# A graph layer on one core: 576 chunks of edges counted in passes of 32 banks instead of 568 in passes of 31, with another plan for interleaving the counted part, and one output buffer instead of two

## The chip, the core and the metric

The kernel runs on one core of one Trainium2 chip. The metric is the device time of one execution in microseconds (us); the number for the kernel before is the median of three runs, 1355.36 us (1352.13 to 1356.22). A profile is one more execution, recorded by the hardware profiler. The engines are PE (TensorE, matrix products; its weight loads are listed apart as PEld), DVE (VectorE), ACT (ScalarE), POOL (GpSimd, which here issues the gathers) and SP (SyncE, which issues most plain transfers).

## What is computed

There are 12,500 nodes with 128 features, 200,000 edges of four types, and one 128x128 weight with a bias for each type:

```python
h = jnp.maximum(_layernorm(x, axis=-1), 0.0)
xs = h[src]
for i in range(4):
    msgs += jnp.where((edge_type == i)[:, None], xs @ W[i] + b[i], 0.0)
return x + jax.ops.segment_sum(msgs, dst, num_segments=12500)
```

The edges are sorted by destination. Destinations are drawn as the square of a uniform number, so the first nodes have very many edges and the last ones few.

## The kernel before

**Chunks.** The edges are cut into 1563 chunks of 128. The first C0 = 568 chunks (all of them edges into about the first 1700 nodes) go the *dense* way, the other TM = 995 the *sparse* way.

**Start.** The normalized features are split into three 16-bit parts and stored to a table in memory, `htab` (98 blocks of 128 rows, 768 bytes a row). Meanwhile the edges of the dense part are sorted into *slots* (`make_slots`). The first three sparse groups (`RAW` = 3, 48 chunks) are gathered from `x` itself, since the table is not ready; part of their work (20 `raw_steps`, emptied three at a time) runs on inside the main loop's first group.

**The sparse way.** The chunks come in groups of G = 16. For each chunk POOL issues one indirect DMA (`gather`, line 591) that brings the 128 rows of its sources from `htab` into a buffer `hm` (10 buffers of two chunks, so at most 20 chunks ahead). DVE builds a one-hot matrix `oh` (line 609), PE multiplies rows by one-hot, three matmuls a chunk (line 644), ACT copies the sums out (line 634), and `weigh` multiplies by the four weights (line 670). DVE adds the result into a ring of running sums (line 733), and finished blocks of 512 nodes leave through `put_out`, `fetch` and `leave`: load `x` (line 751), transpose the ring (line 766), add (line 771), store (line 773). The buffer of this exchange is the tile `xo` of the pool `outp`, which has two buffers.

**The dense way.** For one to three destination nodes at a time, a *bank*, the kernel counts how often each of the 12,500 nodes is a source, by type. A slot (at most 128 edges of a bank) takes two DVE one-hots (`make`, lines 1066, 1070 and 1074) and one matmul of 396 columns (line 1099); ACT turns the counts of a bank into integers (line 1107). Each integer holds three counts as its digits. A *pass* (`multiply`) then multiplies the counts of a batch of banks with the feature table: for each of the 98 table blocks one matmul with the counts read as 8-bit floats and one with counts that ACT decoded (`decode`, line 1167), both of 3 x 4 x banks columns (line 1211). The table blocks stream in through SP (`hs`, line 1195, five buffers of three blocks). UB = 31 is the number of banks in a full batch: 580 banks make 19 batches, the first of 22 and eighteen of 31. The very first pass reads `htab` with three matmuls a block and writes a two-part table `dtab` on the way (`keep`, lines 1181 to 1183), which all later passes read. While a batch is passed, the next one is counted; the first batch has nothing beside it, and the third one (n = 2) is counted alone for its first half, since the pass of the second batch waits for `dtab` (`SETTLE` = 0.5). Where a count runs alone, DVE's one-hots set its pace.

**The order.** PE, DVE and ACT run in the order in which the program is written (`manual_schedule`); SP and POOL are ordered by the scheduler. The main loop (line 1531) goes over the sparse groups from index 3 (`LEAD`) on; between two pieces of a group it takes steps of the generator `dense_work` for as long as the share done is below `pace(gi, part)`. `pace` is a plan in columns: it gives every group the same sum `a_group` of its own columns and dense columns, so that the dense part is done when group FULL - 2 = 58 ends; from index FULL - 1 = 59 on it returns 2.0, which empties whatever is left. Its prices are: 392 columns for a slot, 2.05 x 3 x banks x 392 for a pass and 3.0 x 3 x banks x 392 for the first one.

```python
last = FULL - 1                                  # 1268
a_group = (dense_columns() + sum(own)) / len(own)
...
while work and spent < pace(gi, part):           # 1554
    spent = next(work, None)
```

With TM = 995 there are FULL = 60 groups of 16, then groups of 8, 12, 8, 4 and 3 (index 60 to 64). When the dense part has ended, its memory is freed, buffers `outs` are opened for the last blocks, the four blocks of `acc` (the dense sums) and the blocks still to flush are fetched (lines 1597 to 1608), and the blocks leave while the last groups run.

Of the kernel before, what the change touches and what calls it, by code (L numbers as in the profile page):

```python
# [57 lines left out]
C0 = 568  # L58
UB = 31
# [20 lines left out]
PARTS = 2.05  # L80


@with_exitstack
def kernel(
# [125 lines left out]
    NSLOTS = sum(len(slots_of(u)) for vs in batches for u in vs)  # L210
# [215 lines left out]
    iota_1 = const.tile([P, P], BF16, name="iota_1")  # L426
    nc.vector.tensor_single_scalar(iota_1, iota_b, 1.0, op=ALU.add)
# [25 lines left out]
    ones = const.tile([P, P], F32, name="ones")  # L453
    nc.vector.memset(ones, 1.0)
# [195 lines left out]
    def weigh(t0, g, oh, sb, last):  # L650
# [13 lines left out]
        cnt = spool.tile([P, G * WIN], BF16, name="cnt", bufs=1)[:, : G * win].rearrange("p (g n) -> p g n", g=G)  # L664
# [182 lines left out]
    def check_all():  # L847
# [5 lines left out]
        pb = x_ps.tile([P, 3], F32, name="pt")  # L853
        nc.tensor.matmul(pb, ones, many, start=True, stop=True)
# [19 lines left out]
    def make_slots(dix):  # L874
# [98 lines left out]
        def unpack(a, z, shared):  # L973
# [8 lines left out]
            marks.append(nc.vector.tensor_copy(loT[:, a:z], lo).ins)  # L982
# [59 lines left out]
    def count(now, room):  # L1042
# [18 lines left out]
        def make(n):  # L1061
# [3 lines left out]
            for k, (i, s, by, first, last) in enumerate(sets[n]):  # L1065
# [3 lines left out]
                if by == 1.0:  # L1069
                    one = nc.vector.tensor_scalar(o1[:, k], iota_1, loT[:, s : s + 1], None, ALU.is_equal)  # L1070
                else:
                    if by is None:
                        by = byT[:, s - FIRST : s - FIRST + 1]
                    one = nc.vector.tensor_scalar(o1[:, k], iota_1, loT[:, s : s + 1], by, ALU.is_equal, ALU.mult)  # L1074
# [191 lines left out]
    def pace(gi, part):  # L1266

        last = FULL - 1
        if gi >= last:
            return 2.0  # L1270
        own = [columns(i) for i in range(LEAD, last)]
# [5 lines left out]

    def dense_columns():
        return NSLOTS * float(NB) + sum(3 * len(vs) * (PARTS if i else 3.0) for i, vs in enumerate(batches)) * NW * NT

# [4 lines left out]
    def dense_work():  # L1285


        a_slot = float(NB)
        alone_slot = 3.5 * NB
        a_node = NW * NT  # L1290
        total = dense_columns() + sum(len(slots_of(u)) for u in batches[0]) * (alone_slot - a_slot)
# [3 lines left out]
        for n, vs in enumerate(batches + [None]):  # L1295
# [4 lines left out]
            if vs:  # L1300
                now, first = coming or begin(n)
                coming = None
                steps[first] = sum(len(slots_of(u)) for u in vs) * (a_slot if before else alone_slot)
            if before:
                passed = multiply(before)
                steps[passed] = 3 * len(before[0]) * a_node * (PARTS if before[0] is not batches[0] else 3.0)
# [3 lines left out]
            while done:  # L1310
# [7 lines left out]
                if part is None:  # L1318
                    del done[st]
                    gone += steps[st]  # L1320
# [3 lines left out]
                else:  # L1324
                    done[st] = part
                    yield (gone + sum(done[st] * steps[st] for st in done)) / total
# [432 lines left out]
```

## Time and profile before

| | before |
|---|---|
| median of three runs | 1355.36 us |
| the profiled execution, its own time | 1360.44 us |
| its span in the profile | 1358.7 us |
| busy: PE, PEld | 1243.1 us, 872.8 us |
| busy: DVE, ACT, POOL | 999.0 us, 1066.8 us, 977.8 us |
| gathers from the table (line 591) | 947 |
| slots counted (line 1099) | 1069 |
| casts of counts (line 1107), one for each bank | 580 |

How to read the rows below: a group row gives line, engine, operation, output and inputs by the program's names, the shape, how many (x), the busy time together and the mean of one, and then the idle time just before them with what ended it. A row of windows gives a stretch of time (from and to, in us of the span), its length, and then for each engine the busy time and the number of instructions, the granted PE clock (1.00 is full speed), the share of time in which the DMA engines were busy, and GB/s. A row of waits names who waited, for whom, the total in us, the number of times and the longest. Engine times are as the profiler models them: ends of matmuls overlap, so starts are the safer thing to compare.

### The profile page before, as it was taken

How to read it: one execution, taken by the hardware profiler on the slowest of the kernel's cores; microseconds unless marked ns; L12 is line 12 of the kernel's file. 1: busy time of each engine (PE TensorE's matmuls, PEld its weight loads, DVE VectorE, ACT ScalarE, POOL GpSimd, SP SyncE). 2: the span in 40 equal slices, each digit the busy share in tenths (PEclk: the TensorE clock that was granted, in tenths of full speed). 3: DMA queues.
4: the chain of work that ended last, by engine and by line, in shares of the span. 5: the costliest groups of instructions: out<-in, count | busy, mean ns of one | idle time of the engine just before them, and what ended most of it. 6: DMA issues, size and time to landing. Idle time of an engine off the chain costs nothing.

```text
span 1358.7 us, 30461 instructions
## 1 busy us (share of the span) xinstructions
PE 1243.1 (91%) x9232; PEld 872.8 (64%) x9232; DVE 999.0 (74%) x5139; ACT 1066.8 (79%) x1815; POOL 977.8 (72%) x1024
## 2 busy tenths in 40 slices
PE   5888877999999999999999999999999999998964
PEld 1445654777677766777777676666676666666743
DVE  8996568868888897888776867677676758773552
ACT  6887544889889888898988988888897978886710
POOL 7637463777777777777777777777777777777774
PEclk8885887999999999999999999999999999999977
DMA  7653596888788888888888888887877878778842
GB/s 243 216 204 86 176 338 216 244 272 266 243 256 259 250 255 241 249 257 265 256 259 254 267 249 257 248 246 246 273 227 238 265 214 261 235 234 281 267 122 62
DMA packets 184630, 322.56 MB, mean 237 GB/s; under 512 B 30243, under 2 KB 82524, under 8 KB 184460
## 3 DMA queue, kind: packets, MB, share of 16 engines
q1 hardware_dynamic: 132716, 214.63, 49.0%
q0 software_dynamic: 46992, 96.30, 26.0%
q10 hardware_dynamic: 4752, 9.64, 1.8%
q8 instruction: 73, 1.20, 0.4%
q14 instruction: 97, 0.79, 0.2%
HBM read 294.78 MB, written 25.67 MB: 236 GB/s over the span
## 4 chain that ended last, share of the span: by engine, by line
PE 65%; DMA 12%; DVE 6%; ACT 6%; issue 6%; POOL 4%; DVEq 0%; SPq 0%; ACTq 0%; POOLq 0%
PE pa L1211 35%; PE pt L1099 9%; PE py L670 7%; DMA hm<-htab,srcT 7%; PE ps L644 5%; POOL hm L591 4%; DMA dtab<-dec 2%; DMA hs<-dtab 2%; ACT dec L1167 2%; PE pt L1235 2%; ACT counts L1107 1%; PE ps L702 1%; DVE o L1074 1%; DVE o L1066 1%; PE pt L952 1%
## 5 line engine op out<-in xcount | busy, mean ns | idle before, releaser
L591 POOL DMA_INDIRECT hm<-htab,srcT x947 | 924.3, 976 | 342.1 <-issue 202.5
L1167 ACT ACTIVATE dec<-counts 128x1116 fp32r<-128x1116 uint8 (+1 forms) x594 | 672.2, 1152 | 9.9 <-PE pa L1211 9.0
L1066 DVE TENSOR_SCALAR o<-iota_n,hkT 128x392 bf16<-128x392 f16 x1069 | 354.4, 331 | 180.2 <-PE pt L1099 177.4
L1211 PE MATMUL pa<-dec,hs 128*128 128x372 f32 x1764 | 480.8, 380 | 0.0
L1211 PE MATMUL pa<-counts,hs 128*128 128x372 fp8e4 (+1 forms) x2058 | 435.0, 324 | 22.6 <-DMA hs<-htab 13.8
L1211 PEld LDWEIGHTS pa<-dec,hs 128*128 128x128 f32 x1764 | 309.5, 188 | 41.6 <-issue 0.5
L1107 ACT CAST counts<-pt 128x396 int32<-128x396 f32 x580 | 285.5, 510 | 50.1 <-PE pt L1099 26.2
L1099 PE MATMUL pt<-o,o 128*128 128x396 bf16 x1069 | 285.9, 342 | 15.8 <-ACT counts L1107 9.5
L1211 PEld LDWEIGHTS <-hs 128*128 128x128 f16 (+1 forms) x2058 | 189.6, 98 | 143.1 <-issue 19.4
L644 PE MATMUL ps<-oh,hm 128*128 128x72 bf16 (+7 forms) x2841 | 186.9, 201 | 32.3 <-DMA hm<-htab,srcT 30.9
L1074 DVE TENSOR_SCALAR o<-iota,loT,byT 128x128 bf16<-128x128 bf16 x647 | 216.3, 334 | 0.0
L733 DVE TENSOR_TENSOR ring<-ring,py 128x18 f32 (+6 forms) x912 | 159.0, 174 | 73.1 <-PE py L670 24.1
L644 PEld LDWEIGHTS <-hm 128*128 128x128 f16 x2841 | 136.9, 100 | 103.9 <-DMA hm<-htab,srcT 41.4
L634 ACT ACTIVATE sb<-ps 128x288 f32<-128x288 f32 (+8 forms) x237 | 101.8, 430 | 126.3 <-PE py L670 101.3
L609 DVE TENSOR_SCALAR oh<-iota_b,keyT 128x72 bf16<-128x72 bf16 (+7 forms) x947 | 163.0, 260 | 25.6 <-PE ps L644 24.4
L670 PE MATMUL py<-sb,wsb 128*128 128x288 f32 (+6 forms) x456 | 121.1, 409 | 0.0
L1099 PEld LDWEIGHTS <-o 128*128 128x128 bf16 x1069 | 80.4, 99 | 60.6 <-issue 17.5
L1074 DVE TENSOR_SCALAR o<-iota,loT 128x128 bf16<-128x128 bf16 x422 | 116.7, 277 | 0.0
L670 PEld LDWEIGHTS py<-sb,wsb 128*128 128x128 f32 x456 | 83.3, 193 | 20.7 <-issue 0.3
L575 POOL DMA_INDIRECT hx<-in_x_dram,srcT x48 | 48.0, 1001 | 23.8 <-issue 9.5
L665 ACT CAST cnt<-pt 128x288 bf16<-128x288 f32 (+10 forms) x62 | 25.5, 412 | 39.5 <-PE pt L661 33.6
L509 ACT ACTIVATE h<-hm,nmrt,rstdt 128x128 f32<-128x128 f32 x98 | 42.1, 489 | 0.9 <-DVE mvt L492 0.8
(250 smaller groups left out, 717.8 us busy)
## 6 DMA issues: line engine op xcount, KB each, us to landing
hs<-dtab SPq DMA_DIRECT2D x576, 288.0 KB
hm<-htab,srcT POOLq DMA_INDIRECT x947
htab<-h SPq DMA_DIRECT2D x32, 288.0 KB
hs<-htab SPq DMA_DIRECT2D x32, 288.0 KB
dtab<-dec ACTq DMA_DIRECT2D x32, 288.0 KB
xo<-in_x_dram SPq DMA_DIRECT2D x23, 256.0 KB
out_dram<-xo SPq DMA_DIRECT2D x23, 256.0 KB
hm<-in_x_dram SPq DMA_DIRECT2D x18, 192.0 KB
```

The lines of the kernel that those rows point to most:

```text
L591: one = nc.gpsimd.indirect_dma_start(out=hm[:, (i - h0) * D3 : (i - h0 + 1) * D3], out_offset=None, in_=htab, in_offset=bass.IndirectOffse ...
L609: nc.vector.tensor_scalar(oh[:, i, :], iota_b[:, :K], keyf[:, at : at + 1], None, ALU.is_equal)
L634: nc.scalar.activation(sb[0][:, i0:i1].rearrange("p g t n -> p g (t n)"), ps[:, : i1 - i0, :], AF.Copy, scale=1.0 / UP)
L644: nc.tensor.matmul(ps[:, i - i0, :], rows(i, c), oh[:, i, :], start=(c == 0), stop=(c == 2))
L670: nc.tensor.matmul(py[:, :g, :], wsb[:, t, :], sb[0][:, :g, t, :], start=False, stop=(t == NT - 1))
L733: nc.vector.tensor_tensor(to, to, of(i), ALU.add)
L1066: one = nc.vector.tensor_scalar(o2[:, k, :NB], iota_n, hkT[:, s : s + 1], None, ALU.is_equal)
L1074: one = nc.vector.tensor_scalar(o1[:, k], iota_1, loT[:, s : s + 1], by, ALU.is_equal, ALU.mult)
L1099: one = nc.tensor.matmul(pb, o1, o2, start=first, stop=last)
L1107: lambda i=i, pb=pb: nc.scalar.copy(counts[:, :, i * NT : (i + 1) * NT], pb.rearrange("p (b t) -> p b t", t=NT))
L1167: nc.scalar.activation(decoded[n][:, : j1 - j0, :nv].rearrange("p j (m v) -> p j m v", m=3), by_digit[:, j0:j1, : nu * NT * 4].rearrange(" ...
L1211: nc.tensor.matmul(to if c == 1 and not first else to.rearrange("p (m v) -> p m v", m=3), left, right, start=(j == 0 and c == 0), stop=(js ...
```

## The change

Five things change.

- **More dense chunks, wider passes.** C0 goes from 568 to 576 and UB from 31 to 32. By the formulas of the kernel this makes 596 banks and 1085 slots, still 19 batches (the first of 20 banks, eighteen of 32), and TM = 987 sparse chunks: 60 groups of 16, then 12, 8, 4 and 3. The group of 8 is gone.
- **Another plan.** `pace` runs to `last = FULL`, so the dense part ends with group 59 instead of 58. The prices are new: 4.4 instead of 3.0 for the first pass, 3.5 x 392 for a slot that is counted alone (the first batch, and now also the first half of the third), and 20,000 columns of other work in the loop's first group. The plan now divides by the same total as the work counts itself by.
- **One output buffer.** `outp` has one buffer `xo` instead of two.
- **One-hots compared from 0.** `loT` now holds the low index minus 1, done in the same instruction that converted it, so that `iota_b` serves where `iota_1` (the same plus 1) did; `iota_1` is gone.
- **A table of ones** that only the last check and the fallback path read is made where it is read. A tile of counts, `cnt`, is sized by the widest window in use.

```diff
-C0 = 568
-UB = 31
+C0 = 576
+UB = 32
+FIRST_PASS = 4.4
+ALONE = 3.5
+RAW_WORK = 20000.0
...
-    iota_1 = const.tile([P, P], BF16, name="iota_1")
-    nc.vector.tensor_single_scalar(iota_1, iota_b, 1.0, op=ALU.add)
...
-    ones = const.tile([P, P], F32, name="ones")
-    nc.vector.memset(ones, 1.0)
...
         pb = x_ps.tile([P, 3], F32, name="pt")
+        ones = outp.tile([P, P], F32, name="ones", bufs=1)
+        nc.vector.memset(ones, 1.0)
...
-            marks.append(nc.vector.tensor_copy(loT[:, a:z], lo).ins)
+            marks.append(nc.vector.tensor_single_scalar(loT[:, a:z], lo, -1.0, op=ALU.add).ins)
...
-        last = FULL - 1
+        last = FULL
         if gi >= last:
             return 2.0
-        own = [columns(i) for i in range(LEAD, last)]
+        own = [columns(i) + (RAW_WORK if i == LEAD else 0.0) for i in range(LEAD, last)]
         a_group = (dense_columns() + sum(own)) / len(own)
...
+    def counting_columns(n, part):
+
+        alone = 1.0 if n == 0 else SETTLE if n == 2 else 0.0
+        return sum(len(slots_of(u)) for u in batches[n]) * NB * (part + (ALONE - 1.0) * min(part, alone))
+
+    def passing_columns(n, part):
+        return 3.0 * len(batches[n]) * (PARTS if n else FIRST_PASS) * NW * NT * part
+
     def dense_columns():
-        return NSLOTS * float(NB) + sum(3 * len(vs) * (PARTS if i else 3.0) for i, vs in enumerate(batches)) * NW * NT
+        return sum(counting_columns(n, 1.0) + passing_columns(n, 1.0) for n in range(len(batches)))
...
-                steps[first] = sum(len(slots_of(u)) for u in vs) * (a_slot if before else alone_slot)
+                steps[first] = lambda part, n=n: counting_columns(n, part)
...
-    outp = mid.enter_context(tc.tile_pool(name="outp", bufs=2, side="right"))
+    outp = mid.enter_context(tc.tile_pool(name="outp", bufs=1, side="right"))
```

20 lines of the change are left out of this document (9 added, 11 removed).

## The prediction

> **What bounds the kernel now.** I read the page first, then windows of the gathers, of the matmuls that sum rows, and of all engines, cut where the groups begin; then waits, groups, and the timeline at both ends. From the page:
>
> ```profile
> span 1358.7 us, 30461 instructions
> PE 1243.1 (91%) x9232; PEld 872.8 (64%) x9232; DVE 999.0 (74%) x5139; ACT 1066.8 (79%) x1815; POOL 977.8 (72%) x1024
> PE   5888877999999999999999999999999999998964
> PEclk8885887999999999999999999999999999999977
> L591 POOL DMA_INDIRECT hm<-htab,srcT x947 | 924.3, 976 | 342.1 <-issue 202.5
> ```
>
> PE is full from the eighth slice to the last three, with holes and a lower clock on both sides. POOL looks free by its 72%, but the windows of its gathers (line 591) say otherwise:
>
> ```profile
> 112.00:152.00 40.00, 23.69 (x25) 0.63 0.26 72
> 152.00:262.30 110.30, 63.29 (x62) 0.86 0.82 272
> 262.30:362.00 99.70, 75.92 (x79) 1.00 0.84 262
> 362.00:662.30 300.30, 228.92 (x235) 1.00 0.84 254
> 662.30:1062.30 400.00, 304.32 (x314) 1.00 0.83 251
> 1062.30:1303.70 241.40, 183.16 (x192) 0.98 0.79 243
> 1303.70:1358.70 55.00, 31.34 (x33) 0.69 0.34 90
> ```
>
> From 262 on there is one gather every 1.26 to 1.28 us (400.00 / 314 = 1.274), at the end too, with no room between them; before that one in 1.6 to 1.8. The windows of the summing matmuls (line 644, three a chunk) show the groups:
>
> ```profile
> 112.00:152.00 40.00, 3.39 (x48) 0.63 0.26 72
> 152.00:262.30 110.30, 10.42 (x192) 0.86 0.82 272
> 262.30:362.00 99.70, 12.89 (x240) 1.00 0.84 262
> ...
> 1303.70:1358.70 55.00, 12.46 (x105) 0.69 0.34 90
> ```
>
> 48 matmuls are one group of 16: index 3 takes 40 us, indices 4 to 7 take 110.3 (27.6 each), 8 to 12 take 99.7 (19.9 each). From 362 to 1303.7 lie indices 13 to 59, 941.7 us. The last of them has no dense work:
>
> ```profile
> 1288.85 0.43 PE L644 MATMUL ps<-oh,hm 128*128 128x96 bf16 x6
> ...
> 1301.18 0.95 POOL L591 DMA_INDIRECT hm<-htab,srcT  x1 [0.31 <-issue]
> ...
> 1303.77 0.44 PE L644 MATMUL ps<-oh,hm 128*128 128x104 bf16 x3 [0.46 <-DMA hm<-htab,srcT]
> ...
> 1318.12 3.02 PE L670 MATMUL pt<-sb,wsb 128*128 128x208 f32 x8
> ...
> 1343.85 0.94 POOL L591 DMA_INDIRECT hm<-htab,srcT  x1 [0.30 <-issue]
> ...
> 1351.92 0.44 PE L766 MATMUL pt<-ident,ring 128*128 128x128 f32 x2 [1.68 <-DVE ring L733]
> ```
>
> So 13 to 58 take 1288.7 - 362 = 926.7 us, 20.15 each, and a group of gathers takes 16 x 1.255 (the spacing from 1301.18 to 1343.85, 34 gathers) to 16 x 1.278 (235 in 300.3), 20.1 to 20.4. PE and the gathers run level. The waits of PE's weight loads for gathered rows, in the windows 700 to 900, 900 to 1100 and 1100 to 1285, are small:
>
> ```profile
> PEld L644 <- DMA hm<-htab,srcT: 3.3, 7, 0.8
> ...
> PEld L644 <- DMA hm<-htab,srcT: 7.8, 13, 1.1
> ...
> PEld L644 <- DMA hm<-htab,srcT: 4.7, 5, 2.7
> ```
>
> 15.8 us over the 46 groups, 0.34 each. After 1288.7 no dense work is left to fill PE, and the gathers set the end: the row for index 60 was asked for 2.6 us before PE took it, and the span ends 14.8 us after the last gather.
>
> **The early groups.** By the old plan each group holds 42,611 columns (35,699 dense, 6,912 own), so a planned column costs 20.15 / 42,611 = 0.473 ns in the steady part. Indices 4 to 7 should then take 80.6 us and take 110.3. They hold most of the first pass and the half count that runs alone. The waits of the window 112 to 262 and the one-hots' groups show both:
>
> ```profile
> POOL hm L591 <- PE ps L644: 25.1, 10, 5.0
> PEld L1211 <- DMA hs<-htab: 16.6, 11, 4.3
> ...
> L1066 DVE TENSOR_SCALAR o<-iota_n,hkT 128x392 bf16<-128x392 f16 x1069 | 354.4, 331 | 180.2 <-PE pt L1099 177.4
> ...
> L1074 DVE TENSOR_SCALAR o<-iota,loT,byT 128x128 bf16<-128x128 bf16 x647 | 216.3, 334 | 0.0
> ...
> L1074 DVE TENSOR_SCALAR o<-iota,loT 128x128 bf16<-128x128 bf16 x422 | 116.7, 277 | 0.0
> ```
>
> A slot alone needs 0.61 to 0.67 us of DVE, 1,290 to 1,410 columns at that price, against 392 in the old plan and 1,372 in the new one. The new prices add to indices 4 to 7 about 34,000 columns for the first pass (1.4 x 3 x 22 x 392 less what index 3 did) and 34,300 for the half count, together 32 us; the excess is 29.7. So the new prices fit what those groups cost now.
>
> The new plan gives every group 44,342 columns; index 3 loses 18,269 dense ones (17,430 instead of 35,699). At 0.473 ns that is 8.6 us less for index 3, and indices 4 to 12 take 9 x 20.97 = 188.7 instead of 110.3 + 99.7 = 210.0. Together -30. Following the steps of the generator group by group instead (13 slots in index 3; then 7, 12 and 8 of the 33 steps of the first pass; and so on, each at what such steps take now) I get -26. I take **-28**, bounds 0 (if the rest of the first group's own work, or the clock at 0.63, holds it) and -34. The work is not gone: some 70,000 old-plan columns, 33 us, move behind index 12.
>
> **The steady groups.** 47 groups (13 to 59) now all hold dense work, 1,731 planned columns more each: the wider passes (12 columns more in each of 196 matmuls of a pass), 16 slots more, and the work moved here. The timeline of one pass gives a column's price:
>
> ```profile
> 1286.23 0.81 PE L1211 MATMUL pa<-dec,hs 128*128 128x372 f32 x3
> 1286.88 0.67 PE L1211 MATMUL pa<-counts,hs 128*128 128x372 fp8e4 x3
> 1287.25 0.81 PE L1211 MATMUL pa<-dec,hs 128*128 128x372 f32 x3
> ```
>
> Six matmuls of 372 columns from start to start in 1.02 us, 0.457 ns a column. A group becomes 20.15 + 1.731 x 0.457 - 0.34 (a PE that is slower than the gathers no longer waits for them) = 20.6 us. 47 x 20.6 = 968.2 against 941.7: **+26.5**. Bounds: gathers at 1.255 set the floor, 47 x 20.08, +2; every planned column at 0.473 and no wait recovered gives 20.97, +44. I choose between them by the rows of the passes, which are most of the work.
>
> The Trainium skill, "TensorE: Matmul & The Clock Gate", section "Back-to-back issue gap", gives a warm matmul N / 2.4 ns plus a fixed 2.5 ns. By it an added column costs 0.417 ns, the fixed part nothing, and this term would be +23 instead of +26.5; the row's 0.457 holds also what is fixed per matmul, so it is an upper price for columns that only lengthen matmuls.
>
> The other engines cover their share. ACT and DVE in the window from 362 (busy PE, PEld, DVE, ACT, POOL):
>
> ```profile
> 362.00:662.30 300.30, 294.30 (x2356) 213.21 (x2355) 249.69 (x1303) 265.10 (x419) 228.92 (x235) 1.00 0.84 254
> ...
> 1303.70:1358.70 55.00, 31.76 (x203) 22.23 (x203) 18.41 (x89) 5.79 (x14) 31.34 (x33) 0.69 0.34 90
> ```
>
> ACT is at 88%. 4.8% more dense columns a group (37,430 for 35,699) in 2.2% more time make it 90.5%, DVE 85%: hidden under PE; if ACT bound instead, a group would cost 20.15 x 1.048 = 21.1, just over the upper bound above. The table is streamed 19 times as before, so the DMA load per pass stays.
>
> **The end.** From the start of index 60 the kernel needed 55.0 us for 8 + 12 + 8 + 4 + 3 = 35 chunks. Now 27 are left there, and with PE setting the pace up to index 59 POOL is further ahead: at most 20 chunks (7 x 1.255 + 14.8 = 24 us to the end), or 8 if it only keeps some 10 us (19 x 1.255 + 14.8 = 39). PE itself was busy 31.8 us in that window; less the eight chunks (8 / 35 of the 12.46 us that the same window of line 644 has, 2.8, and the 3.0 us product of that group at 1318) it needs about 26, and with the 6.8 us that follow its last matmul, 33. I take 37, **-18**; bounds 33 (-22) and 45 (only the eight gathers saved, -10).
>
> **One output buffer, and the rest.** A fetch already waits for the store ahead of it to land:
>
> ```profile
> 490.97 0.39 SPq L773 DMA_DIRECT2D out_dram<-xo  x1
> ...
> 495.08 0.38 SPq L751 DMA_DIRECT2D xo<-in_x_dram  x1
> ```
>
> 4.1 us, behind which the table loads of line 1195 queue on SP; PE, five buffers (15 blocks, 30 matmuls, about 5 us) ahead, mostly covers it. With one buffer the fetch waits for the same store. Two places are new. The sums of the raw groups hold the one buffer until their adds in indices 4 to 6 are done, so the first block's fetch, and the table loads behind it, wait for DVE there: 0 to 4 us, taken as 1. At the end, the block due at index 59 is flushed at 61, after the late buffers were dealt out at 60, so its fetch needs one of theirs back: a store and a fetch, 4 to 8 us, while line 771's add holds DVE and behind it the ring adds, one-hots and then PE. The last gathers hide most of it; 1, and 8 without that cover. The removed `iota_1` and `ones` are two short DVE instructions ahead of the loop, `loT`'s subtraction rides in an instruction that exists, 16 more slots widen the slot building by 1.5%: 0. Together **+2**, bounds 0 and 8.
>
> **Sum.** -28 + 26.5 - 18 + 2 = -17.5 on the profiled execution's own 1360.44 us (1.7 outside the span): 1342.9. That execution is 0.4% over the median of the runs; scaled by 1355.36 / 1360.44 the time is **1338 us**, 1.3% faster.
>
> **Rivals.**
> (B) *The gathers set the pace, PE's added columns vanish under them.* For it: the unbroken spacing above, and PE's waits for rows. Against it: PE would have to do 4% more in the same 20.4 us while it is 98% busy. The last gather then comes 28 us earlier for the early groups and 8 x 1.274 = 10.2 earlier for the chunks saved: -38, 1317. The skill's "Perfetto Trace Analysis", section "GPSIMD Engine Instruction", says to time this engine by the spacing of starts, not by its busy span; the windows agree (1.274 us from start to start against a mean of 0.976 busy).
> (C) *The early groups do not get shorter* (the slower side). Place: indices 3 to 12. If the raw steps, the table's round trip through `dtab` and the waits for `hs` set these 250 us rather than the amount of dense work, the thinner plan only pushes 33 us behind. Price 0 instead of -28: +26.5 - 18 + 2 = +10.5, 1366. It decides once less than 10.5 us is gained there. Against it: the excess of 29.7 us that the new prices explain, and 25.1 us in which POOL waited for PE there.
> (D) *The columns cost full price*, 20.97 a group: -28 + 44 - 18 + 2 = 0, 1355. For it: this is the mean price of a planned column now. Against it: that mean holds fixed costs and waits.
> That the plan does not do what it says is a part of D: if dense work slipped past index 59 or the late block stalled the end, the end's gain would be gone, -17.5 + 18, again about 1355.
>
> **Chances.** Forecast 0.62 (its own range 1320 to 1352), B 0.20, C 0.10, D 0.08. About 0.3% is what a measurement of this kernel can tell from no change. Faster: 0.60 of the forecast and B, 0.80; same: D's 0.06 and 0.02 of the forecast, 0.08; slower: C and the rest of D, 0.12. The range 1312 to 1362 takes in most of B and D and leaves out C's centre, and nearly 0.2 in all.
>
> **What would show it.** Index 13 should start near 334 instead of 362, with POOL at 1.28 us a gather from about 230 on; from there 20.6 us a group and hardly a wait for gathered rows; index 60 near 1302, and 37 us from there to the end. If the gathers stay unbroken and PE waits for rows, it is B; if indices 3 to 12 still take 250 us, C; if a group takes 21 us, D. The forecast is wrong if two of the three terms miss by over 10 us in the same direction.

## The result, and the profile after

The changed kernel takes 1347.68 us (median of 20 runs, 1343.2 to 1357.92), the kernel before beside it 1355.64 us (20 runs, 1350.91 to 1359.79): a ratio of 0.9956 with a 95% interval of 0.9938 to 0.9974. It is faster by 0.4%, where 1.3% was forecast. The profiled execution of the change took 1353.06 us, 0.4% over its median, as the one of before was over its own. From the page after:

```profile
span 1351.3 us, 30386 instructions
PE 1248.1 (92%) x9211; PEld 878.6 (65%) x9211; DVE 999.3 (74%) x5154; ACT 1086.2 (80%) x1828; POOL 966.1 (71%) x1016
PE   4878876899999999999999999999999999999995
PEclk9985798789999999999999999999999999999997
L589 POOL DMA_INDIRECT hm<-htab,srcT x939 | 913.3, 973 | 336.2 <-issue 216.3
```

PE stays full to the last slice but one, where before it thinned out over three. The low digits of PE and of its clock at the start are still there. The windows of all engines, cut where each group's first summing matmul starts (from, to, length, then busy PE, PEld, DVE, ACT, POOL, granted PE clock, DMA share, GB/s), are those of index 3, indices 4 to 6 together, each of 7 to 12, indices 13 to 59, and the end:

```profile
108.80:145.20 36.40, 31.34 (x169) 26.04 (x169) 12.97 (x62) 23.79 (x66) 21.54 (x23) 0.50 0.28 73
145.20:211.20 66.00, 50.34 (x488) 38.33 (x487) 49.81 (x233) 34.31 (x85) 47.80 (x48) 0.95 0.86 292
211.20:235.20 24.00, 13.90 (x114) 9.12 (x113) 18.96 (x91) 7.82 (x20) 15.40 (x15) 0.77 0.83 279
235.20:259.80 24.60, 20.85 (x126) 13.61 (x124) 20.69 (x112) 14.18 (x24) 18.50 (x21) 0.67 0.41 110
259.80:278.70 18.90, 18.74 (x154) 13.09 (x152) 17.37 (x89) 17.30 (x28) 14.47 (x15) 1.00 0.86 259
278.70:305.30 26.60, 23.66 (x167) 17.14 (x166) 9.75 (x54) 18.94 (x26) 16.65 (x18) 0.87 0.84 260
305.30:327.00 21.70, 20.93 (x164) 15.05 (x164) 18.28 (x92) 18.74 (x30) 15.47 (x16) 1.00 0.74 219
327.00:345.70 18.70, 18.70 (x152) 13.34 (x151) 15.22 (x78) 17.36 (x28) 14.28 (x15) 1.00 0.84 253
345.70:1313.20 967.50, 947.65 (x7190) 674.71 (x7188) 720.17 (x3762) 845.02 (x1288) 726.68 (x753) 1.00 0.83 251
1313.20:1351.30 38.10, 23.47 (x178) 18.95 (x176) 16.12 (x86) 4.94 (x12) 9.25 (x10) 0.81 0.27 78
```

| | before | forecast | the change's profile |
|---|---|---|---|
| up to index 3 | 112.1 us | | 108.8, -3.3 |
| indices 3 to 12 | 250.0 us | -28 | 236.9, **-13.1** |
| indices 13 to 59 | 941.7 us | +26.5 | 967.5, **+25.8** (20.58 a group) |
| from index 60 | 55.0 us | -18 | 38.1, **-16.9** |
| span | 1358.7 us | -17.5, with +2 for the rest | 1351.3, -7.4 |

Two of the three large terms came out as forecast. The early one came out at half its size. In the rows above the long groups have places: index 3 ran at half clock from end to end (0.50), and indices 7, 8 and 10 took 24.0, 24.6 and 26.6 us at 0.77, 0.67 and 0.87, while 9 and 12 beside them took 18.9 and 18.7 at full clock.

PE sets the pace of the steady part alone. In the waits of weight loads from 345.7 to 1288 the wait for gathered rows is gone but for crumbs (total, times, longest):

```profile
PEld L642 <- DMA hm<-htab,srcT: 7.4, 46, 0.2
```

At the end the late block does wait for its load as forecast, in the waits from 1313.2 on and in SP's queue, but the stores behind it still take 14.3 us to be issued:

```profile
DVE xo L769 <- DMA xo<-in_x_dram: 5.2, 1, 5.2
```

```profile
1325.70 0.39 SPq L771 DMA_DIRECT2D out_dram<-xo  x1
1328.03 0.38 SPq L749 DMA_DIRECT2D xo<-in_x_dram  x1
1331.54 14.32 SPq L771 DMA_DIRECT2D out_dram<-xo  x6
```

### The profile page after: what moved, and what is told of

Same layout as the page of the kernel before. It is cut to its first block, busy times and chain, and to the rows that moved or that the text cites. A ratio compares the mean times of both kernels' runs of the same rounds, so it can differ in the third digit from the quotient of the medians.

```text
span 1351.3 us, 30386 instructions
## 1 busy us (share of the span) xinstructions
PE 1248.1 (92%) x9211; PEld 878.6 (65%) x9211; DVE 999.3 (74%) x5154; ACT 1086.2 (80%) x1828; POOL 966.1 (71%) x1016
## 4 chain that ended last, share of the span: by engine, by line
PE 79%; DVE 8%; ACT 6%; DMA 4%; issue 3%; DVEq 0%; SPq 0%; ACTq 0%
PE pa L1211 43%; PE pt L1099 11%; PE py L668 8%; PE ps L642 6%; ACT dec L1167 2%; PE pt L1235 2%; DVE ring L731 2%; PE ps L700 1%; DMA hs<-dtab 1%; DMA hs<-htab 1%; ACT counts L1107 1%; PE pt L952 1%; DVE o L1074 1%; DVE o L1066 1%; PE pt L659 1%
## 5 line engine op out<-in xcount | busy, mean ns | idle before, releaser
L1167 ACT ACTIVATE dec<-counts 128x1152 fp32r<-128x1152 uint8 (+1 forms) x594 | 692.9, 1190 | 7.5 <-PE pa L1211 6.9
L1211 PE MATMUL pa<-dec,hs 128*128 128x384 f32 x1764 | 493.1, 387 | 0.0
L1211 PE MATMUL pa<-counts,hs 128*128 128x384 fp8e4 (+1 forms) x2058 | 440.2, 327 | 26.7 <-DMA hs<-htab 16.3
L1099 PE MATMUL pt<-o,o 128*128 128x396 bf16 x1085 | 290.8, 340 | 21.0 <-ACT counts L1107 11.5
L1211 PEld LDWEIGHTS <-hs 128*128 128x128 f16 (+1 forms) x2058 | 189.1, 98 | 148.1 <-issue 22.7
L1074 DVE TENSOR_SCALAR o<-iota_b,loT,byT 128x128 bf16<-128x128 bf16 x663 | 221.9, 335 | 0.0
L731 DVE TENSOR_TENSOR ring<-ring,py 128x14 f32 (+6 forms) x912 | 158.6, 174 | 61.2 <-issue 16.1
L632 ACT ACTIVATE sb<-ps 128x224 f32<-128x224 f32 (+7 forms) x235 | 102.3, 436 | 122.6 <-PE py L668 109.1
L607 DVE TENSOR_SCALAR oh<-iota_b,keyT 128x56 bf16<-128x56 bf16 (+7 forms) x939 | 160.9, 262 | 22.9 <-PE ps L642 22.9
L642 PE MATMUL ps<-oh,hm 128*128 128x56 bf16 (+7 forms) x2817 | 176.5, 200 | 0.0
L668 PE MATMUL py<-sb,wsb 128*128 128x224 f32 (+6 forms) x456 | 122.6, 413 | 0.0
L1074 DVE TENSOR_SCALAR o<-iota_b,loT 128x128 bf16<-128x128 bf16 x422 | 114.2, 271 | 0.0
L663 ACT CAST cnt<-pt 128x224 bf16<-128x224 f32 (+10 forms) x61 | 25.8, 422 | 24.3 <-PE pt L659 20.8
L507 ACT ACTIVATE h<-hm,nmrt,rstdt 128x128 f32<-128x128 f32 x98 | 42.2, 492 | 0.8 <-DVE mvt L490 0.7
```

What stands on the lines that cost most here:

```text
L607: nc.vector.tensor_scalar(oh[:, i, :], iota_b[:, :K], keyf[:, at : at + 1], None, ALU.is_equal)
L632: nc.scalar.activation(sb[0][:, i0:i1].rearrange("p g t n -> p g (t n)"), ps[:, : i1 - i0, :], AF.Copy, scale=1.0 / UP)
L642: nc.tensor.matmul(ps[:, i - i0, :], rows(i, c), oh[:, i, :], start=(c == 0), stop=(c == 2))
L668: nc.tensor.matmul(py[:, :g, :], wsb[:, t, :], sb[0][:, :g, t, :], start=False, stop=(t == NT - 1))
L731: nc.vector.tensor_tensor(to, to, of(i), ALU.add)
L1074: one = nc.vector.tensor_scalar(o1[:, k], iota_b, loT[:, s : s + 1], by, ALU.is_equal, ALU.mult)
```

## Experiments

In four of the six sets of runs every kernel was some 20% slower (the kernel before took 1617 to 1639 us there, 1356 to 1357 in the other two), so each ratio below is to the kernel before in the same set, and times are compared within a set only.

| kernel | us | before beside it | ratio, 95% interval |
|---|---|---|---|
| plan_only | 1605.8 | 1639 | 0.9799, 0.9768 to 0.983 |
| size_only | 1623.27 | 1639 | 0.9906, 0.9873 to 0.9939 |
| fetch_pool | 1626.69 | 1639 | 0.9906, 0.9872 to 0.9941 |
| one_buffer | 1639.22 | 1639 | 0.9994, 0.9975 to 1.0014 |
| change_again | 1348.27 | 1356.95 | 0.9937, 0.9915 to 0.9958 |
| **plan_only_2** | **1334.22** | 1356.95 | **0.9822, 0.9796 to 0.9848** |
| fetch_pool_2 | 1354.31 | 1356.95 | 0.9979, 0.9964 to 0.9994 |
| plan_pool | 1360.28 | 1356.95 | 1.0024, 1.0006 to 1.0041 |
| **plan_one_buf** | **1333.54** | 1356.15 | **0.982, 0.979 to 0.9851** |
| change_two_buf | 1354.46 | 1356.15 | 0.9971, 0.9944 to 0.9997 |
| prices_only | 1338.0 | 1356.15 | 0.9865, 0.984 to 0.9891 |
| size_only_2 | 1353.91 | 1356.15 | 0.9986, 0.9969 to 1.0003 |
| change_third | 1612.5 | 1637.4 | 0.9868, 0.9829 to 0.9906 |
| late_flush | 1615.36 | 1637.4 | 0.9881, 0.9838 to 0.9923 |
| raw_30000 | 1608.75 | 1637.4 | 0.9829, 0.9788 to 0.9869 |
| late_flush_2 | 1613.69 | 1631.97 | 0.9876, 0.9839 to 0.9913 |
| raw_30000_2 | 1608.25 | 1631.97 | 0.9836, 0.9797 to 0.9875 |
| raw_30000_3 | 1580.36 | 1616.74 | 0.9777, 0.9753 to 0.9802 |

Where the profile was taken in one of the two quicker sets, the groups' starts give these segments (worked out as in the table above):

| kernel | 3 to 12 | 13 to 59 (one group) | from 60 |
|---|---|---|---|
| before | 250.0 | 941.7 (20.04) | 55.0 |
| the change, its first profile | 236.9 | 967.5 (20.58) | 38.1 |
| change_again | 226.7 | 965.3 (20.54) | 38.8 |
| change_two_buf | 236.3 | 964.9 (20.53) | 39.7 |
| fetch_pool_2 | 230.9 | 964.6 (20.52) | 45.9 |
| plan_only_2 | 219.8 | 950.9 (20.23) | 48.9 |
| plan_one_buf | 221.3 | 950.9 (20.23) | 49.1 |
| prices_only | 228.4 | 954.8 (20.31) | 45.7 |
| plan_pool | 218.4 | 963.9 (20.51) | 61.3 |
| size_only_2 | 264.0 | 935.8 (19.91) | 44.5 |

### Which of the edits does it

plan_only is the kernel before with nothing but the new plan: 568 chunks, 31 banks and two output buffers stay.

```diff
+FIRST_PASS = 4.4
+ALONE = 3.5
+RAW_WORK = 20000.0
...
-        last = FULL - 1
+        last = FULL
```

(with `counting_columns`, `passing_columns` and the sums that use them, as in the change). size_only is the rest, on the old plan:

```diff
-C0 = 568
-UB = 31
+C0 = 576
+UB = 32
...
-    outp = mid.enter_context(tc.tile_pool(name="outp", bufs=2, side="right"))
+    outp = mid.enter_context(tc.tile_pool(name="outp", bufs=1, side="right"))
```

(with the one-hots from 0, the table of ones and `cnt`). one_buffer is the kernel before with only the last two of these lines. The one-hots from 0, the table of ones and `cnt` have no run of their own, nor are C0 and UB taken apart: what is called the size below is all of these together.

> The kernel before with the new plan alone (dense part spread to index 59, new prices, 568 chunks, 31 banks, two buffers). If the gain of the change comes from the plan (early groups less full, the end's gap filled), indices 3 to 12 lose 16 to 20 us, a steady group costs 20.3 instead of 20.15 us (+12 over 47 groups), the end from index 60 falls from 55 to about 47: 1338 to 1343 us, ratio 0.988 to 0.991, better than the whole change. If the gain comes from the eight gathers saved, the plan alone gives nothing: ratio 0.998 to 1.002.

> 576 chunks, 32 banks and one buffer with the old plan (dense part to index 58, old prices). If the plan makes the gain, the early groups still take 250 us, 46 dense groups cost 0.3 us more each (+14), the end is shorter by the eight gathers (-10): ratio 1.000 to 1.005. If the eight gathers make it: ratio 0.990 to 0.994.

> The kernel before with one output buffer instead of two and nothing else. If a fetch waits for the store ahead of it with one buffer as with two, only the first block is late (its buffer is held by the raw sums): 0 to 5 us more, ratio 1.000 to 1.004. If one buffer costs a stall at each of the 18 blocks in the loop, 2 us each: ratio 1.02 or more.

> The kernel before with the new plan alone, a second time. If the gain of the change is the plan's and the added dense columns give part of it back: faster than the whole change, ratio 0.985 to 0.992, index 13 some 16 to 20 us earlier than before, 20.3 us a group, 47 us from index 60 on. If the eight gathers saved are what pays: 0.998 to 1.002.

> 576 chunks, 32 banks and one buffer with the old plan, a second time. If PE's added columns and the one buffer cost what the eight gathers save: early groups 255 to 260 us, 20.3 us a dense group, 40 to 45 us from index 60 on: ratio 0.998 to 1.004. If the size pays by itself as on the first chip (0.9906): 0.988 to 0.994.

> The changed kernel itself, beside the three others. If this chip runs the kernel before at about 1355 us: ratio 0.994 to 0.998, index 13 near 346 us, 20.6 us a group, 38 us from index 60 to the end. If it runs it at about 1640 us, as the chip of the first four did, the plan gave 0.980 and the size 0.991 there: 0.970 to 0.975 if the two add up, 0.985 to 0.99 if they do not.

The plan alone is 1.8% faster, about three times the whole change beside it (0.6%), and better than was expected of it both times; the size alone cannot be told from no change in the quicker set (0.9986) and gains 0.9% in the slower one; one buffer alone does nothing (0.9994). The windows of plan_only_2, cut at the same borders but with 11 and 12 together, show what the plan does by itself (index 9 is left out):

```profile
112.10:148.40 36.30, 31.24 (x169) 25.99 (x169) 13.84 (x65) 22.92 (x65) 21.52 (x24) 0.50 0.29 77
148.40:210.50 62.10, 49.14 (x452) 35.69 (x451) 49.04 (x234) 32.15 (x80) 46.79 (x47) 0.89 0.83 278
210.50:231.40 20.90, 14.92 (x140) 10.77 (x139) 14.61 (x65) 7.52 (x19) 14.26 (x16) 0.92 0.99 348
231.40:249.40 18.00, 12.38 (x96) 7.78 (x96) 17.55 (x99) 10.22 (x23) 13.73 (x15) 0.81 0.49 160
...
270.60:290.20 19.60, 19.60 (x161) 14.52 (x160) 13.30 (x74) 18.36 (x29) 14.82 (x16) 1.00 0.88 276
...
331.80:1282.70 950.90, 933.85 (x7212) 671.05 (x7210) 718.34 (x3754) 830.59 (x1282) 723.71 (x746) 1.00 0.84 256
1282.70:1331.60 48.90, 28.90 (x215) 22.55 (x213) 19.30 (x105) 6.09 (x15) 26.48 (x28) 0.77 0.36 97
```

Indices 3 to 12 take 219.8 us, 30.2 less than before. Indices 7, 8 and 10 take 20.9, 18.0 and 19.6, the three that take 24.0, 24.6 and 26.6 in the change; they do not hold quite the same steps, so sums of groups compare better than single ones. A steady group costs 0.35 us less than in the change, and the end 10.8 more: these two are the size's, 47 x 0.35 = 16.6 against 10.8.

The size alone, in the windows of size_only_2 (early, steady, end), loses early with the old plan too:

```profile
108.40:372.40 264.00, 230.44 (x1731) 168.58 (x1730) 188.72 (x931) 188.68 (x353) 162.44 (x167) 0.86 0.72 227
372.40:1308.20 935.80, 912.74 (x6990) 650.95 (x6989) 698.68 (x3656) 810.96 (x1239) 711.20 (x738) 1.00 0.82 250
1308.20:1352.70 44.50, 25.47 (x166) 18.00 (x166) 15.10 (x69) 4.56 (x11) 23.47 (x25) 0.73 0.34 94
```

14 us more in the early groups than before (264.0 to 250.0), 10.5 less at the end. So with either plan the size loses early: 14 with the old one, 7 to 17 with the new. Index 3 differs with the clock; without it, indices 4 to 12 take 183.5 and 185.0 us in plan_only_2 and plan_one_buf, and 194.5 to 200.8 in the four profiles with the new plan and the wide size. The steady groups differ: 14 us more had been expected for them, and they take 5.9 less than before (935.8 and 941.7). PE was busy 5.6 us longer there (912.74 and 907.13) and idle 11.5 us less. With the old plan the added columns went into PE's idle time; in plan_only_2 only 17 us of it are left in the steady groups, and there the columns cost time.

Three more kernels split the plan and cross the buffers. plan_one_buf is plan_only with one buffer, prices_only is plan_only that ends a group earlier, change_two_buf is the change with two buffers, which cost two of the ten buffers of gathered rows:

```diff
plan_one_buf, against plan_only
-    outp = mid.enter_context(tc.tile_pool(name="outp", bufs=2, side="right"))
+    outp = mid.enter_context(tc.tile_pool(name="outp", bufs=1, side="right"))
prices_only, against plan_only
-        last = FULL
+        last = FULL - 1
change_two_buf, against the change
-    hpool = mid.enter_context(tc.tile_pool(name="rows", bufs=10))
+    hpool = mid.enter_context(tc.tile_pool(name="rows", bufs=8))
-    outp = mid.enter_context(tc.tile_pool(name="outp", bufs=1, side="right"))
+    outp = mid.enter_context(tc.tile_pool(name="outp", bufs=2, side="right"))
```

> The new plan alone (568 chunks, 31 banks) with one output buffer instead of two. If the one buffer is what the early groups of the changed kernel lost (its first fetch waits for the store ahead of it while the table loads queue behind it on SP): indices 3 to 12 rise from 219.8 to 226 to 232 us, the kernel is 6 to 10 us slower than the plan alone: ratio 0.986 to 0.990. If the loss comes with the 32 banks: 0.980 to 0.984, as the plan alone.

> The new plan alone, but with the dense part ending at index 58 as before (`last = FULL - 1`). If the later end fills the gap at index 59: the early groups stay at 220 us, a dense group costs 20.5 us, and the kernel is 9 to 14 us slower than the plan alone: ratio 0.989 to 0.993. If the later end is worth nothing: 0.980 to 0.984.

> The changed kernel with two output buffers; the room comes from eight row buffers instead of ten (16 chunks ahead instead of 20). If the one buffer costs the early groups: indices 3 to 12 fall from 227 to 237 to 218 to 224 us and the ratio is 0.985 to 0.990. If it is the size: the ratio stays within 0.003 of the changed kernel's 0.9937.

One buffer is free with this plan too (0.982 beside 0.9822), and two do not help the change (0.9971; its 8 row buffers are a second difference, which no run takes apart). The prices give 1.35% and the later end another 0.3 to 0.45%, with intervals that just overlap (1338.0 and 1333.5 us in the same set; 9 to 14 us had been expected): prices_only loses 8.6 us in the early groups and 3.9 in the steady ones against plan_only_2, and has 3.2 back at the end.

### Why the early groups lose with the wider size

**The first pass.** The wide size leaves the first batch 20 banks instead of 22, and the plan counts its pass by banks: 2 x 3 x 4.4 x 392 = 10,349 columns less, 4.8 us at the 0.464 ns that a planned column costs in the steady groups (20.23 us / 43,631 for the plan alone, 20.58 / 44,342 = 0.464 for the change). The plan fills that room with other work. But with the new plan the pass does not get shorter. Its 294 matmuls, asked for by their line over the stretch of the first pass, in plan_only_2 (duration in ns, least, median and longest; first and last start; then PE's idle time before them and the number of times):

```profile
L1213 PE MATMUL pa<-counts,hs x294: 277/279/428, 157.6 to 228.3; 128*128 128x264 fp8e4 x147
...
  DMA hs<-htab: 10.6, 8
```

and in the change's profile:

```profile
L1211 PE MATMUL pa<-counts,hs x294: 266/268/408, 153.3 to 225.5; 128*128 128x240 fp8e4 x147
...
  DMA hs<-htab: 16.3, 13
```

Each matmul is 11 ns shorter, 3.2 us together, and PE waits 5.7 us longer for the table's blocks: 72.2 us from the first to the last start instead of 70.7. These two are the ends of a spread, but the others agree. With the new plan and 22 banks (plan_one_buf, prices_only and plan_pool beside plan_only_2) the waits are 9.1 to 14.0 us and the stretch 70.7 to 72.7; with 20 banks (change_again, change_two_buf and fetch_pool_2 beside the change) they are 14.9 to 19.3 and 71.6 to 76.2. In indices 5 and 6 of the change's profile the DMA engines are busy 0.98 and 1.02 of the time. So the arrival of the blocks paces much of this pass, and two banks less turn matmul time into waiting. With the old plan the stretch is 2.8 us shorter in size_only_2 (65.7) than before (68.5), but fewer other matmuls stand in it there (102 summing ones instead of 114, 16 weighing ones instead of 24).

**The store and the load.** In the change one block of nodes leaves in index 10, where 16 of the 33 steps of the second pass run with only 2 counts beside them. SP's queue of the change's profile there:

```profile
284.76 0.43 SPq L771 DMA_DIRECT2D out_dram<-xo  x1
287.01 0.32 SPq L1195 DMA_DIRECT2D hs<-dtab  x1
289.76 0.38 SPq L749 DMA_DIRECT2D xo<-in_x_dram  x1
290.26 5.22 SPq L1195 DMA_DIRECT2D hs<-dtab  x6
```

The load of `x` waits 5.0 us for the store, the table blocks behind it wait too, and PE runs dry:

```profile
293.90 0.69 PE L1211 MATMUL pa<-counts,hs 128*128 128x384 fp8e4 x3 [1.19 <-DMA hs<-dtab]
...
296.88 1.14 PE L1211 MATMUL pa<-counts,hs 128*128 128x384 fp8e4 x3 [1.76 <-DMA hs<-dtab]
```

In the plan alone the same exchange falls one group later, in index 11, since with the smaller C0 the block is done eight chunks later in the sparse order. There the load waits 4.3 us and PE only 0.6 for table blocks, in a group of 22.6 us at full clock:

```profile
290.20:312.80 22.60, 21.25 (x171) 15.70 (x169) 12.72 (x66) 18.51 (x28) 17.32 (x18) 1.00 0.91 285
```

```profile
294.56 0.39 SPq L775 DMA_DIRECT2D out_dram<-xo  x1
...
298.82 0.38 SPq L753 DMA_DIRECT2D xo<-in_x_dram  x1
```

So indices 10 and 11 have to be taken together: 42.2 us in plan_only_2 and 42.6 in plan_one_buf, 48.3 in the change's profile and 45.9 in change_again. After the exchange before this one PE waits for table blocks in index 7 too, 6.4 us in the change's profile and 6.6 in change_again, but also 4.5 in plan_only_2 and 6.6 in plan_one_buf, so that wait is hardly the size's. fetch_pool takes the load out of this queue, in the change; plan_pool does so in plan_only.

```diff
-            nc.sync.dma_start(xt[:, :nf, :], x[j0 * P : (j0 + nf) * P, :].rearrange("(j p) d -> p j d", p=P))
+            nc.gpsimd.dma_start(xt[:, :nf, :], x[j0 * P : (j0 + nf) * P, :].rearrange("(j p) d -> p j d", p=P))
```

> The changed kernel, with the load of x for a finished block issued by POOL instead of SP, so that its wait for the store ahead of it no longer holds the table loads on SP. If that wait is what the early groups lost against the forecast, indices 7 and 10 fall from 24.0 and 26.6 us to about 20 to 21 and the whole is 7 to 11 us faster than the changed kernel: ratio to the kernel before 0.987 to 0.991. If the loss lies in work that the plan prices too low (the raw groups in index 3, slots counted alone), it stays at 0.994 to 0.997.

> The changed kernel with the load of x for a finished block on POOL's queue, a second time. If the wait on SP behind the store (5.0 us at 208 and at 285 us) is what indices 7 and 10 lost: they fall from 24.0 and 26.6 us to 20 to 22, and the kernel is 6 to 11 us faster than the whole change run beside it. If they stay within 1 us, the loss lies elsewhere (DVE's one-hots, cold clock) and the ratio equals that of the whole change within 0.003.

> The new plan alone on the kernel before, with that load on POOL's queue too. If both edits pay on their own: 3 to 8 us faster than the plan alone, ratio 0.980 to 0.988 and the fastest of the four. If POOL's own time for the load (some 1 us each, 19 times) and its wait cost the gathers as much: equal to the plan alone or slower.

The windows of indices 7 and 10 and of the end in fetch_pool_2:

```profile
216.30:237.70 21.40, 14.96 (x115) 10.02 (x113) 17.12 (x81) 7.48 (x20) 13.94 (x14) 0.74 0.90 285
...
279.70:301.70 22.00, 21.10 (x167) 15.56 (x165) 9.31 (x54) 18.97 (x26) 16.09 (x18) 1.00 0.96 305
...
1306.80:1352.70 45.90, 23.72 (x177) 18.89 (x176) 16.14 (x86) 4.94 (x12) 17.82 (x19) 0.76 0.29 82
```

Index 10 falls from 24.2 (change_again) or 26.6 to 22.0, index 7 from 23.7 or 24.0 to 21.4. Indices 10 and 11 together take 43.7, and PE's wait for table blocks in index 10 falls from 2.9 or 3.1 us to 0.9. But the kernel as a whole loses: 18 gathers and a load (x19 of POOL) are left for the end instead of 10 gathers, and it takes 7.8 us more than in the change's profile. Each of the 26 loads takes 0.57 to 0.83 us of POOL itself, and around one the gathers of the steady groups come some 2.05 us apart instead of 1.28, mostly without a wait for the store. In plan_pool, whose gathers had less lead, a steady group takes 20.51 us instead of 20.23 and the end 61.3 instead of 48.9, where the late block waits for its load, and the gain of the plan is gone (1.0024):

```profile
DVE xo L773 <- DMA xo<-in_x_dram: 24.9, 1, 24.9
```

late_flush moves that one block a group later in the change, to where the plan alone has it:

```diff
         for ja, _, c in flushes
     ]
+    goes[2] += 1
```

> The changed kernel, with the block of nodes that leaves through the output buffer in index 10 (store, then a load that held SP 5.0 us while PE did 16 steps of a pass with 2 counts) due one group later, in index 11, where 30 counts stand beside the pass. If the early loss of the wide passes is this meeting of a store and a nearly pure pass (theory F), index 10 falls from the 24 to 27 us of three profiles to 20 to 21.5, index 11 stays under 23, indices 3 to 12 end 4 to 5 us earlier for the same index 3, and the ratio to the kernel before is about 0.990 to 0.993 against 0.9937 to 0.9956. If index 10 is long by its own work (16 steps of a pass of 32 banks, PE alone: theory W), it stays at 24 or more and the time does not change. If the wait only moves, index 11 grows by what index 10 loses.

> late_flush once more, since the chip of the first run is slower for every kernel (1637 us for the kernel before). There index 10 fell by 3 us and index 11 grew by 7: if that holds (the wait of the load for the store moves with the block and is not covered in index 11 either), here index 10 is 20 to 22, index 11 25 to 29 instead of 21.7, and the ratio is that of the change or worse, 0.994 to 0.998. By theory F it was 0.990 to 0.993.

> The change itself once more, as what the other two of this call are compared with: ratio 0.9937 to 0.9956 to the kernel before; indices 3 to 12 between 226 and 237 us, index 10 at 24 us or more.

change_third is the change in the same set. Its windows of indices 10 and 11:

```profile
320.20:347.70 27.50, 24.07 (x168) 17.09 (x166) 10.57 (x57) 20.78 (x28) 16.51 (x18) 0.88 0.83 256
347.70:369.40 21.70, 20.93 (x164) 15.06 (x164) 17.23 (x89) 16.92 (x27) 13.73 (x15) 1.00 0.71 204
```

and those of late_flush:

```profile
318.00:342.40 24.40, 21.61 (x163) 15.08 (x162) 8.75 (x53) 20.57 (x29) 15.20 (x16) 1.00 0.77 246
342.40:371.40 29.00, 23.98 (x170) 17.26 (x169) 19.42 (x95) 18.96 (x29) 16.81 (x17) 0.88 0.65 197
```

Index 10 loses 3.1 us and index 11 gains 7.3 (late_flush_2: 25.2 and 28.2), and the time did not fall. In index 10 PE's wait for table blocks falls from 2.9 us to 1.1 and 1.3, as it does in fetch_pool (1.0), so there the exchange did cost time. But the longer index 11 is not the wait moved on: PE waits for no table block in it, and fetch_pool, in a slower set too and with the block still leaving in index 10, has the same long index 11 at the same clock:

```profile
320.40:344.50 24.10, 22.03 (x167) 15.59 (x165) 9.38 (x52) 20.10 (x28) 14.99 (x16) 1.00 0.83 264
344.50:373.30 28.80, 24.47 (x167) 16.82 (x166) 18.73 (x96) 19.22 (x30) 17.18 (x18) 0.88 0.65 191
```

What makes index 11 long in these runs is open, and with it what a later exchange would be worth in a quicker set.

**The place of the counts that run alone.** raw_30000 gives the loop's first group less dense work, so that indices 7 to 10 hold nearly what they hold in plan_only:

```diff
-RAW_WORK = 20000.0
+RAW_WORK = 30000.0
```

> The changed kernel with RAW_WORK = 30000 instead of 20000: 7 counts of the first batch move from index 3 to 4, and the contents of indices 7 to 10 come to lie nearly as in the plan alone (index 7: 7 steps of the first pass, 2 and 11 counts; index 8: 27 counts, 2 steps; index 10: 14 steps, 7 counts instead of 16 and 2). Theory P (the loss of the early groups is the position of the counts that run alone against the group borders, so chance of the constants): indices 7 to 12 fall from 129.5 to 134.4 us to 122 to 126, the time falls by 4 to 8 us, ratio 0.988 to 0.992. Theory W (32 banks simply cost it): indices 3 to 12 stay at 227 to 237, ratio 0.993 to 0.997.

> raw_30000 once more, for the same reason. Theory P: indices 7 to 12 at 122 to 126 us and the ratio 0.988 to 0.992. Theory W: indices 7 to 12 at 129 or more, indices 3 to 12 at 227 to 237, ratio 0.993 to 0.997.

> raw_30000 a third time; the first two met the condition in which the kernel before takes 1632 to 1637 us, and gained 1.6 to 1.7% there against 1.3% of the change itself. Theory P: if the kernel before takes about 1356 us here, indices 7 to 12 at 122 to 126 us and the ratio 0.988 to 0.992. Theory W: indices 7 to 12 at 129 or more, ratio 0.993 to 0.997. If it is 1630 again, the ratio should be 0.983 as twice before.

Indices 7 to 12 take 148.1, 149.7 and 147.6 us against 148.8 in change_third: their contents moved, their sum did not. The ratio is lower than the change's in all three (0.9829, 0.9836 and 0.9777 against 0.9868), but the first two intervals overlap that of change_third and the third run was in a set of its own. All three fell into the slower sets, so what it does at 1356 us stays open.

**The clock.** The three longest places of the change's profile have a lower granted clock than the same places in change_again, whose windows of indices 3, 7, 8 and 10 are:

```profile
109.80:141.20 31.40, 26.33 (x170) 21.68 (x170) 13.27 (x62) 23.39 (x66) 21.46 (x23) 0.62 0.30 82
...
207.00:230.70 23.70, 13.70 (x114) 8.79 (x112) 18.13 (x87) 7.94 (x20) 14.45 (x15) 0.76 0.82 280
230.70:252.50 21.80, 17.85 (x127) 11.44 (x126) 20.58 (x110) 14.27 (x25) 16.62 (x18) 0.79 0.42 111
...
271.90:296.10 24.20, 21.14 (x168) 15.63 (x166) 9.60 (x55) 18.86 (x26) 18.20 (x20) 1.00 0.91 288
```

It is the same program with the same matmuls (170 and 169 in index 3): 31.4 us at 0.62 against 36.4 at 0.50, 21.8 at 0.79 against 24.6 at 0.67, 24.2 at 1.00 against 26.6 at 0.87. Together 10.2 us, all of the difference between these two profiles in indices 3 to 12 (236.9 and 226.7). PE's idle time is the same in both, within 0.2 us in each of the three (5.1, 3.8 and 4.0, 2.9 and 3.1); what grew is the busy time of the same matmuls.

## Why the prediction was wrong

**The early groups: the step that failed.** "I take -28" was made of 8.6 us for index 3 and of "indices 4 to 12 take 9 x 20.97 = 188.7 instead of 110.3 + 99.7 = 210.0". For the plan alone it was right: 30.2 us less, and 183.5 us in indices 4 to 12 of plan_only_2. For the changed kernel the two profiles give -13.1 and -23.3, with 200.5 and 195.3 us in indices 4 to 12, 22.3 and 21.7 a group instead of 20.97. The step that failed is this price: the forecast charged the wider size there by its planned columns, as in the steady groups. From the plan's 219.8 us the runs lead to the change's time so:

- planned columns, 711 more in each of ten groups at 0.464 ns: +3.3.
- the room that two banks less make in the first pass on paper and not on the clock, an estimate from the rows above: +4.8.
- the exchange, which the plan alone covers in index 11 and the change does not in index 10: 2.2 to 4.6 from fetch_pool_2's 22.0. The forecast had seen this wait and let five table buffers "mostly" cover it.

That makes 230 to 233 us. fetch_pool_2 without the third term should have 227.9 and has 230.9; change_two_buf has 236.3 and the change's profile 236.9, 4 to 7 over it; change_again has 226.7, with 5.0 of it won in index 3 by the clock. What is left over is of the size of the clock's own variation; how the rest divides is not settled.

That change_again comes out near the forecast is in part luck. It is the fastest of its 12 executions (1342.29 us, median 1348.27), and its index 13 starts at 336.5, its index 60 at 1301.8, 38.8 us before the end, where 334, 1302 and 37 were forecast. The change's first profile is 5.4 us over the median of its 20. What a usual execution loses of the 28 us most likely lies between the two, between 5 and 15. All terms are taken against one profile of the kernel before, 5 us over its own median, and where that one spent the 5 us is not known.

The bound 0, "if ... the clock at 0.63, holds it", was the right place to look: index 3, forecast at 31.4, took 31.4 at 0.62 and 36.4 at 0.50.

The Trainium skill, "TensorE: Matmul & The Clock Gate", section "Part 1: The HAM clock gate", says that the array runs at half speed when idle and at full speed after some 3.4 us of sustained work, with a window that runs freely, so that it differs from run to run. The difference from run to run is there (31.4 and 36.4 us); the other half did not hold in index 3 of the change's profile, where PE was busy 31.34 of 36.40 us, as the profile models it, 12.1 us of it without a break, and the clock stayed at 0.50.

**The steady groups: right.** +25.8 and +23.6 in two profiles for +26.5; 20.58 and 20.54 us a group for 20.6; and 7.4 us of waits for gathered rows, "hardly a wait". The first pass is on the side of the forecast's 0.457 ns a column: 24 columns less made 11 ns, 0.46 ns a column, by the profile's modelled durations. The Trainium skill's rule for back-to-back matmuls (same page, "Back-to-back issue gap"), which the page gives for matmuls by themselves, has 0.417 ns; by it the term was +23, as near to the two profiles as +26.5, so they do not decide between the two.

**The end: right.** -16.9 and -16.2 for -18, at 38.1 and 38.8 us for 37. plan_only_2 shows the parts: with the plan and without the eight gathers saved the end takes 48.9 us, so about 6 us are the plan's and 10.8 the size's, near the 10 that the forecast had for "only the eight gathers saved".

**One buffer and the rest: +2 forecast, about 0.** One buffer alone makes 0.9994; beside the plan it changes 0.9822 into 0.982. The small edits that came with it were not run by themselves. The late block waited 5.2 us as forecast and its cover held. Index 3 starts 3.3 us earlier in the change's profile, but prices_only and plan_pool, which have none of these edits, start it at 109.0 and 109.4 too, so this is no effect of theirs.

**The rivals.** B fell: POOL now waits for PE (its lead at the starts of the groups stays at 20 to 27 us from index 13 to 59), and 753 gathers in 967.5 us are one in 1.285. C fell by sign, the early groups did get shorter. D's price of 20.97 did not come, 20.58 did; its total, 1355, was 7 us off on the other side, for another reason. What was missing among the rivals is that a planned column can cost differently in the first pass: a plan counts by banks what comes at the pace of table blocks.

**The version that beats both** is the plan alone, with one buffer or two: 1333.5 to 1334.2 us, 1.8% under the kernel before. The wider size adds 14 to 17 us to a PE that is full and 7 to 17 us early, and saves 10 at the end.

## What to carry to other kernels

Test the halves of a change that mixes a better plan with a larger size: here the plan gave 1.8%, and the size gave about two thirds of it back. A plan in units of work is right only where that unit sets the pace; where a stage is paced by a transfer, making it smaller frees nothing, and the plan fills room that is not there. A load that waits for a store should not stand in a queue that feeds the engine setting the pace, and moving it to another queue helps only if the engine that issues it there has time to spare.

## What the runs showed of the hardware that was not expected

**A program ran 21% slower for whole sets of runs, and not by the chip alone.** One chip gave 1356.15 us for the kernel before in one set and 1637.4 in a later one. The costliest weight loads by groups, in the kernel before:

```profile
L1211 PEld LDWEIGHTS <-hs 128*128 128x128 f16 (+1 forms) x2058 | 189.6, 98 | 143.1 <-issue 19.4 <-DMA hs<-htab 16.6 <-DMA hs<-dtab 5.0
```

and in one_buffer, which equals it but for a buffer, in a slower set:

```profile
L1211 PEld LDWEIGHTS <-hs 128*128 128x128 f16 (+1 forms) x2058 | 192.4, 100 | 215.5 <-issue 103.2 <-DMA hs<-htab 11.6 <-DMA hs<-dtab 9.6
```

The instruction takes as long as before (100 and 98 ns); what grew is the time before it in which the profile shows nothing that PE waited for, 103.2 us against 19.4. What it is stays open. Gains and losses there are not those of the quicker sets: size_only has 0.9906 there and 0.9986 in the other. A steady group takes 24.8 us in plan_only and 24.9 in change_third, so there the wider size costs 0.16 us a group and not 0.35.

**Two executions of one and the same program differ by 10 us with the granted clock**, in groups in which PE has holes: 0.50 or 0.62 over the whole of index 3, where the busy time of the same matmuls is 31.3 or 26.3 us and the idle time 5.1 in both.
